# Layers 2 and 3 of a four-layer convolution network: TensorE's products pinned to alternate between pairs of the two layers

## The chip, the cores and the metric

The kernel runs on one core of one Trainium2 chip. The metric is the device time of one execution in microseconds (us). Names of engines: PE is TensorE's matmuls, PEld its weight loads, DVE is VectorE, ACT ScalarE, POOL GpSimd, SP the engine that issues most transfers. L1002 means line 1002 of the kernel.

## The reference

The input x has the shape (4, 8, 512, 512): four time steps t, eight channels, images of 512 x 512. Four layers follow each other, each of the form x + f(gn(x)), where gn normalises each group of two channels of an image to mean 0 and variance 1.

```python
x = x + _L0_conv_ref(_gn(x), ...)             # spiking attention
x = x + _L1_conv_ref(_gn(x), L1_conv_w)       # 13 x 13 depthwise convolution
x = x + _L2_conv_ref(_gn(x), L2_conv_weight, L2_conv_bias)   # quantised 3 x 3
x = x + _L3_conv_ref(_gn(x), L3_conv_weight, L3_conv_bias)   # plain 3 x 3
```

Only layers 2 and 3 matter here. Layer 2 rounds its normalised input to integers between -127 and 127, convolves it with rounded weights and scales the result back:

```python
qx = _quantize(x, sx); qw = _quantize(weight, sw)
out = conv3x3(qx, qw) / (sx * sw) + bias
```

Layer 3 is `conv3x3(gn(x), weight) + bias`. Its normalisation needs the mean and variance over the whole image of layer 2's output at this t, so layer 3 of a t can only begin when layer 2 of that t is done.

## The kernel before

Layers 0 and 1 run first and leave their result in device memory (x2d). The function `layers23` then does layers 2 and 3 together. An image of 512 rows is cut into 85 windows of 8 rows, with 8 channels each: 64 partitions hold one window, 128 hold two. A tile k is up to two windows; a *pair* p is two such tiles, so up to four windows. There are 22 pairs in each t (`N_PAIRS`), 88 in all, and the last pair of a t is smaller.

One loop, over n, goes through all pairs. Iteration n does, in the order of the program:

- `load`: the transfer of pair n+5 into SBUF, on SP's queue;
- `normalise` of pair n+2: POOL copies x into u in another order of columns (L967), ACT normalises it into y (L971);
- `quantise` of pair n+1: DVE rounds y into xq (L982), one of three buffers;
- `layer2` of pair n: for each of the two tiles six products of 64 x 64 by 64 x 512 in bf16 (L1002) into one of three PSUM buffers; then DVE scales them and adds u, writing layer 2's output into the ring x3 (L1009), and either ACT squares it with a running sum (L1015) or DVE takes its statistics (L1020);
- from time to time `halos`: transfers on POOL's queue inside x3, which give each window the border rows of its neighbours (L1154);
- `layer3` of pair n-25 (22 pairs of one t plus `LAG` = 3): POOL fills two edge columns (L1097), PE does 24 products of 64 x 64 by 64 x 512 in f32 (L1104) into two of four PSUM buffers, ACT adds the constant (L1113), and SP stores the output (L1120).

The ring x3 holds 26 pairs (`RING`). Pair n of layer 2 is written where pair n-26 was, so the eviction at L1009 may not start before layer 3 has read pair n-26. That is a dependency that the framework finds by itself.

After the last pair of a t the steps of `norm3` are spread over the next iterations: sums on DVE, two products that add over partitions (L178, in `group_steps`), a power on POOL (L195), the scaled weights of layer 3 (L1073), and a product that gives its constant (L1082).

Each engine works through its own queue in a fixed order. The framework sets that order when the program is built, from the order of the program and an estimate of when each instruction becomes ready, so instructions may stand in another order than they are written in. `tc.issue_after(op)` ties this down: each instruction traced in the block stands behind `op` on the engine of `op`. It adds no semaphore and no wait for another engine. In the kernel before, `normalise` and `quantise` stand behind the last DVE and ACT operations of the layer 2 before (the dictionary `done`), layer 2 stands behind `normalise` and `quantise` on their own engines, and layer 3's products stand behind layer 2's of the same iteration (`did`). Nothing ties layer 2's products of the next iteration to layer 3's of this one.

Of the kernel before, what the change touches and what calls it, by code (L numbers as in the profile page):

```python
# [78 lines left out]
def windows(k):  # L79

    p, j = divmod(k, 2)
    every = [(a, 4 * p + 2 * j + (a ^ j)) for a in range(2)]
    return [(a, q) for a, q in every if q < W_ALL]
# [813 lines left out]
def layers23(  # L897
    s, tc, x2d, out, ident, ind, mask2, avg_same, group_steps, m2, r2, most, w, early, pool
):
    nc = tc.nc  # L900
# [36 lines left out]
    def tiles(p):  # L937
        return [k for k in (2 * p, 2 * p + 1) if k < W2_N]

    def slot(t, p):  # L940
        return 2 * ((t * N_PAIRS + p) % RING)
# [3 lines left out]
    def load(t, p):  # L945
        ahead[t, p] = xt = early["x"].tile([P, 2, D], F32, tag="x", name=f"x2_{t}_{p}")
        src = x2d[t]
        first, second = (dict(windows(k)) for k in (2 * p, 2 * p + 1))
        for a, q in first.items():

            n = 2 if a in second else 1
            step = second[a] - q if n == 2 else 1
            nc.sync.dma_start(
                xt[a * HALF : (a + 1) * HALF, :n, :],
                bass.AP(
                    src.tensor, src.offset + q * W_STEP * B * D,
                    [[D, HALF], [step * W_STEP * B * D, n], [1, D]],
                ),
            )

    def normalise(t, p):
        n, n_p = len(tiles(p)), HALF * len(windows(tiles(p)[-1]))
        x = ahead.pop((t, p))[:n_p, :n, :]
        u = early["u"].tile([P, 2, D], F32, tag="u", name="u2")
        y = early["y"].tile([P, 2, D], F32, tag="y", name="y2")
        for j in range(n):
            nc.gpsimd.tensor_copy(  # L967
                u[:n_p, j, :].rearrange("p (v g) -> p v g", g=PH),
                x[:, j, :].rearrange("p (g v) -> p v g", g=PH),
            )  # L970
        op = nc.scalar.activation(  # L971
            y[:n_p, :n, :], u[:n_p, :n, :], AF.Identity, bias=w["mr"][:n_p, t : t + 1],
            scale=w["r"][:n_p, t : t + 1],
        )
        ready[t, p] = u, y[:n_p, :n, :]
        return op.ins

    def quantise(t, p):
        u, y = ready[t, p]
        n_p, n, _ = y.shape  # L980
        xq = w["xq"][(t * N_PAIRS + p) % 3]
        op = nc.vector.tensor_scalar(  # L982
            xq[:n_p, :n, 2 : D + 2], y, ROUND, ROUND, op0=ALU.add, op1=ALU.subtract
        )
        ready[t, p] = u, xq
        return op.ins
# [4 lines left out]
    def layer2(t, p):  # L991
        ks = tiles(p)
        n_p = HALF * len(windows(ks[-1]))
        u, xq = ready.pop((t, p))
        s0 = slot(t, p)
        st3 = w["st3"][t % 2]
        for j, k in enumerate(ks):
            ps = ps_2.tile([P, D], F32, tag="conv2", name="ps_conv2")
            for dx in range(3):
                for a, _ in windows(k):  # L1000
                    half = slice(a * HALF, (a + 1) * HALF)
                    mm = nc.tensor.matmul(  # L1002
                        ps[half, :], lhsT=w["band2"][half, 0, dx, :], rhs=xq[half, j, dx + 1 : dx + 1 + D],
                        start=dx == 0, stop=dx == 2,
                    )
            own = x3[:n_p, s0 + j, 1 : D + 1]
            sums = w["sums"][t % 2][:, :, k : k + 1]
            summed = k in by_sums(t)
            done["DVE"] = nc.vector.scalar_tensor_tensor(  # L1009
                own, ps[:n_p, :], w["inv"][:n_p], u[:n_p, j, :], op0=ALU.mult, op1=ALU.add,  # L1010
                accum_out=sums[:, 0, :] if summed else None,
            ).ins
            if summed:
                square = wpool.tile([P, D], BF16, tag="square", name="square")
                done["ACT"] = nc.scalar.activation(  # L1015
                    square, own, AF.Square, bias=w["m"][:, t : t + 1], scale=-1.0,
                    accum_out=sums[:, 1, :],
                ).ins
            else:
                done["DVE"] = nc.vector.bn_stats(st3[:n_p, k, :], own).ins  # L1020
        return mm.ins
# [3 lines left out]
    def halos(t, p0, p1):  # L1025


        for c in range(4):
            first = max(p0, 1) if c == 0 else p0
            n = min(p1, (W_ALL - c + 3) // 4) - first  # L1030
            _, j, a = place(c)
            before, j_b, a_b = place(c + 3)
            for q0, q1, n_q in split(t, first, n, before - 1):
                here = pairs[a * HALF : (a + 1) * HALF, q0 : q0 + n_q, j, :]
                there = pairs[a_b * HALF : (a_b + 1) * HALF, q1 : q1 + n_q, j_b, :]
                end = (W_IN - 1) * B
                yield here[:B], there[W_STEP * B : (W_STEP + 1) * B]
                yield there[end : end + B], here[B : 2 * B]
# [51 lines left out]
    def layer3(t, p, zero, band, const):  # L1090


        ks = tiles(p)
        s0 = slot(t, p)
        n_p = HALF * len(windows(ks[-1]))
        edge = x3[:n_p, s0 : s0 + len(ks), 0 : D + 2 : D + 1]
        nc.gpsimd.tensor_copy(edge, zero[:n_p].unsqueeze(2).to_broadcast([n_p, len(ks), 2]))  # L1097
        ps = [ps_3.tile([P, D], F32, tag="conv3", name="ps_conv3") for _ in ks]
        for dx in range(3):
            for j, k in enumerate(ks):  # L1100
                for a, q in windows(k):
                    half = slice(a * HALF, (a + 1) * HALF)
                    b = 1 if q == W_ALL - 1 else a ^ j
                    nc.tensor.matmul(  # L1104
                        ps[j][b * HALF : (b + 1) * HALF, :], lhsT=band[half, b, dx, :],
                        rhs=x3[half, s0 + j, dx : dx + D],
                        start=dx == 0, stop=dx == 2,
                    )
        for j, k in enumerate(ks):
            q = 4 * p + 2 * j  # L1110
            used = slice(HALF if q == W_ALL - 1 else 0, P)
            o = early["o"].tile([P, D], F32, tag="o", name="o3")
            nc.scalar.activation(o[used], ps[j][used], AF.Identity, bias=const[used])  # L1113
            row, n = q * W_STEP + 1, 2 * W_STEP
            at = 2 * B
            if q == 0:
                row, n, at = row - 1, n + 1, at - B
            if q == W_ALL - 1:
                n, at = W_STEP + 1, HALF
            nc.sync.dma_start(  # L1120
                out[t, :, row : row + n, :].rearrange("c r w -> r c w"), o[at : at + n * B, :]
            )

    n_chunk = N_PAIRS // 2
    copies, at_once = [], 0
    n_all = T * N_PAIRS
    norms, norm, done = {}, iter(()), {}
    for n in range(n_all + N_PAIRS + LAG):  # L1130
        if n < n_all:
            for m in range(6) if n == 0 else [n + 5]:
                if m < n_all:
                    load(*divmod(m, N_PAIRS))


            with ExitStack() as order:
                for op in done.values():
                    order.enter_context(tc.issue_after(op))
                for m in range(3) if n == 0 else [n + 2]:  # L1140
                    if m < n_all:
                        first = normalise(*divmod(m, N_PAIRS))
                for m in range(2) if n == 0 else [n + 1]:
                    if m < n_all:
                        then = quantise(*divmod(m, N_PAIRS))
            with tc.issue_after(first), tc.issue_after(then):
                did = layer2(*divmod(n, N_PAIRS))
        next(norm, None)
        if n_chunk < n <= n_all + 3 and n % n_chunk == 3:
            t, p = divmod(n - 3 - n_chunk, N_PAIRS)  # L1150
            copies = list(halos(t, p, p + n_chunk))
            at_once = -(-len(copies) // (n_chunk - 2))
        for _ in range(min(at_once, len(copies))):
            nc.gpsimd.dma_start(*copies.pop(0))  # L1154
        if n >= N_PAIRS + LAG:
            t, p = divmod(n - N_PAIRS - LAG, N_PAIRS)
            with tc.issue_after(did):
                layer3(t, p, *norms[t])
        if n < n_all and n % N_PAIRS == N_PAIRS - 1:
            norm = norm3(n // N_PAIRS)  # L1160
        next(norm, None)
# [36 lines left out]
```

## Time and profile before

| | |
|---|---|
| time, median of 3 | 3056.27 us (3052.8 to 3060.18) |
| profiled span | 3049.7 us |
| layer 0 | 0 to about 2116 us |
| layer 1 | 2116 to about 2595 us |
| layer 2 alone (25 pairs) | 2595 to 2678 us |
| layers 2 and 3 together | 2678 to 2970 us |
| layer 3 alone (25 pairs) | 2970 to 3049.7 us |
| PE busy over the span | 2917.8 us, 96% |
| DVE, ACT, POOL busy | 73%, 18%, 34% |

The page cuts the span into 40 equal slices of about 76 us; each digit is the busy share of a slice in tenths. Shares over the whole span hide the stage in question, since layer 0 alone takes two thirds of it; the views that count are those by stretches of time. The DMA share is the mean busy share of the core's 16 DMA engines. A wait is written as "engine, what waited, <- what released it: total us, times, longest us".

### The profile page before, as it was taken

To read this page: it belongs to the slowest core of one execution; us is meant where nothing else is said; L and a number is where in the kernel's file an instruction comes from. 1 tells how busy PE (TensorE), PEld (TensorE's weight loads), DVE (VectorE), ACT (ScalarE), POOL (GpSimd) and SP (SyncE) were. 2 spreads that over 40 slices of the span, in tenths; PEclk is the share of its full clock that TensorE was granted. 3 is DMA by queue.
4 is the path that set the end of the run, shared out by engine and by line. 5 is a ranking of instruction groups with operands and counts; after the bars stand their busy time and mean duration, and the time that the engine had idled before them with its cause. 6 is when DMAs were issued, how large, how long until landed. Compare 5 with 4: busy or idle time off the path is not lost. (4 is left out here: it accounts for less than half of the span.)

```text
span 3049.7 us, 38814 instructions
## 1 busy us (share of the span) xinstructions
PE 2917.8 (96%) x13993; PEld 1459.2 (48%) x13993; DVE 2223.0 (73%) x3793; ACT 554.2 (18%) x867; POOL 1042.9 (34%) x1963
## 2 busy tenths in 40 slices
PE   8999999999999999999999999998999999678989
PEld 6555555555555555555555555554433333234434
DVE  5997688688779868868876876886455556967860
ACT  1400010010000001000001000100111111756664
POOL 1242233333234323323322432333111112766751
PEclk9999999999999999999999999998999999799999
DMA  5222222222222222122221111112877878888986
GB/s 181 80 81 64 77 63 64 70 63 70 70 63 63 71 65 76 60 67 63 63 70 43 57 50 50 57 36 73 212 215 204 217 202 226 147 181 203 229 189 160
DMA packets 275702, 327.37 MB, mean 107 GB/s; under 512 B 23600, under 2 KB 171192, under 8 KB 275285
## 3 DMA queue, kind: packets, MB, share of 16 engines
q1 hardware_dynamic: 211930, 235.77, 29.0%
q0 software_dynamic: 23776, 62.35, 7.5%
q10 hardware_dynamic: 39803, 26.77, 3.0%
q8 instruction: 110, 1.80, 0.3%
q14 instruction: 83, 0.68, 0.1%
HBM read 210.60 MB, written 103.17 MB: 103 GB/s over the span
## 5 line engine op out<-in xcount | busy, mean ns | idle before, releaser
L464 PE MATMUL ps_in<-w_v,xn 128*128 128x512 f32 x1024 | 461.4, 599 | 2.4 <-issue 2.1
L464 PE MATMUL ps_in<-w_k,xn 128*128 128x512 f32 x1024 | 450.2, 593 | 1.1 <-DVE v_k L429 0.8
L464 PE MATMUL ps_in<-xn,w_q 128*128 128x512 f32 x1024 | 449.6, 592 | 0.1
L750 PE MATMUL ps_conv<-x,bt 112*64 112x512 f32 x2048 | 444.5, 593 | 0.0
L500 PE MATMUL ps_b<-toep,vtok 128*64 128x512 bf16 x3072 | 369.8, 381 | 0.0
L412 ACT ACTIVATE h_q<-v_q,c_half 128x512 f32<-128x512 f32 x96 | 69.3, 722 | 1543.6 <-DVE v_q L408 1184.1
L549 POOL COPY x1s<-x1s 128x2 f32<-128x2 f32 (+1 forms) x1024 | 226.7, 275 | 296.0 <-DVE x1s L538 296.0
L437 POOL TENSOR_TENSOR h_v<-h_v,c_v 128x512 f32<-128x512 f32 x96 | 123.1, 1282 | 575.3 <-DVE h_v L436 540.7
L527 PE MATMUL ps_out<-wp,so 128*128 128x512 f32 x1024 | 308.9, 444 | 0.0
L464 PEld LDWEIGHTS ps_in<-w_k,xn 128*128 128x128 f32 x1024 | 194.1, 190 | 222.5 <-issue 205.0
L464 PEld LDWEIGHTS ps_in<-xn,w_q 128*128 128x128 f32 x1024 | 191.8, 190 | 220.0 <-issue 213.1
L464 PEld LDWEIGHTS ps_in<-w_v,xn 128*128 128x128 f32 x1024 | 190.0, 190 | 216.4 <-issue 210.9
L750 PEld LDWEIGHTS ps_conv<-x,bt 112*64 112x64 f32 x2048 | 149.9, 135 | 286.0 <-issue 285.5
L500 PEld LDWEIGHTS <-vtok 128*64 128x64 bf16 x3072 | 208.6, 110 | 123.1 <-issue 1.6
L1104 PE MATMUL ps_conv<-x,band_t 64*64 64x512 f32 x2040 | 265.9, 609 | 0.0
L967 POOL COPY u<-x 128x512 f32<-128x512 f32 (+1 forms) x172 | 203.9, 1219 | 109.3 <-issue 66.2
L527 PEld LDWEIGHTS ps_out<-wp,so 128*128 128x128 f32 x1024 | 192.6, 188 | 94.1 <-issue 58.3
L1002 PE MATMUL ps_conv<-xq,band 64*64 64x512 bf16 x1020 | 144.9, 409 | 65.6 <-DVE xq L982 53.6
L538 DVE SCALAR_TENSOR_TENSOR x1s<-v_p,xr 128x256 f32<-128x256 f32 x256 | 186.6, 769 | 14.9 <-DMA x<-x1s 3.6
L766 POOL DMA_DIRECT2D x<-xo x128 | 71.4, 564 | 339.9 <-ACT xo L757 325.4
L1009 DVE SCALAR_TENSOR_TENSOR x<-ps_conv,inv,u 128x512 f32<-128x512 f32 (+1 forms) x172 | 123.1, 743 | 84.6 <-PE ps_conv L1104 64.4
L195 POOL TENSOR_TENSOR grstd_x<-grstd_x,neg_half 128x1 f32<-128x1 f32 (+1 forms) x28 | 22.3, 796 | 462.2 <-DVE grstd_x L194 462.2
(182 smaller groups left out, 3609.4 us busy)
## 6 DMA issues: line engine op xcount, KB each, us to landing
x<-x SPq DMA_DIRECT2D x64, 917.0 KB
x<-x SPq DMA_DIRECT2D x168, 256.0 KB
x<-x1s POOLq DMA_DIRECT2D x128, 262.0 KB, 2.6
x<-in_x SPq DMA_DIRECT2D x128, 256.0 KB
xr<-in_x SPq DMA_DIRECT2D x128, 256.0 KB
out<-o SPq DMA_DIRECT2D x164, 192.0 KB
xs<-in_x SPq DMA_DIRECT2D x112, 256.0 KB
x<-xo ACTq DMA_DIRECT2D x128, 128.0 KB
```

The lines of the kernel that those rows point to most:

```text
L437: nc.gpsimd.tensor_add(h, h, c_twice[n])
L464: mm = nc.tensor.matmul(ps, lhsT=lhsT, rhs=rhs, start=k == 0, stop=k == NC - 1)
L500: nc.tensor.matmul(pb[two * DH : (two + 1) * DH, :], lhsT=v[:, c, h * DH : (h + 1) * DH], rhs=toep[z][:, h, u : u + N], start=c == 0 and z ...
L527: nc.tensor.matmul(ps, lhsT=so[:, k, c * P : (c + 1) * P], rhs=wpT[z][:, k, :], start=k == 0 and z == 0, stop=k == NC - 1 and z == 1,)
L538: nc.vector.scalar_tensor_tensor(own, v.rearrange("p (g v) -> p g v", g=PH)[:, two, :], 1.0, by_phase[:, two, :], op0=ALU.is_ge, op1=ALU.add,)
L549: nc.gpsimd.tensor_copy(x1[:, f, u : u + n], x1[:, fm, um - n + 1 : um + 1][:, ::-1])
L750: nc.tensor.matmul(ps[q * M1 : (q + 1) * M1, :], lhsT=bt[:, z, :], rhs=xt[:, w0 : w0 + N_PS1, z : z + NV], start=z == 0, stop=z == SHIFTS - 1,
L766: engine.dma_start(bass.AP(dst.tensor, dst.offset + (q * n_half * W1_OUT * B + b) * D + f * NV, [[B * D, W1_OUT], [W1_OUT * B * D, n_half] ...
L967: nc.gpsimd.tensor_copy(u[:n_p, j, :].rearrange("p (v g) -> p v g", g=PH), x[:, j, :].rearrange("p (g v) -> p v g", g=PH),)
L1002: mm = nc.tensor.matmul(ps[half, :], lhsT=w["band2"][half, 0, dx, :], rhs=xq[half, j, dx + 1 : dx + 1 + D], start=dx == 0, stop=dx == 2,)
L1009: done["DVE"] = nc.vector.scalar_tensor_tensor(own, ps[:n_p, :], w["inv"][:n_p], u[:n_p, j, :], op0=ALU.mult, op1=ALU.add, accum_out=sums[ ...
L1104: nc.tensor.matmul(ps[j][b * HALF : (b + 1) * HALF, :], lhsT=band[half, b, dx, :], rhs=x3[half, s0 + j, dx : dx + D], start=dx == 0, stop= ...
```

## The change

Layer 3 now returns its last product, and layer 2's instructions of the next iteration are traced behind it, in addition to `normalise` and `quantise`. Since layer 3 was already tied behind layer 2 of its own iteration, PE's products of this stage are now in one fixed order: the pair of layer 2 of iteration n, the pair of layer 3 of iteration n, the pair of layer 2 of iteration n+1, and so on. Only PE's queue is bound by it. In the first 25 iterations there is no layer 3 yet and `behind` is empty. The purpose is to keep PE from running layer 2 ahead of layer 3.

```diff
@@ layer3
-                    nc.tensor.matmul(
+                    mm = nc.tensor.matmul(
                         ps[j][b * HALF : (b + 1) * HALF, :], lhsT=band[half, b, dx, :],
...
                 out[t, :, row : row + n, :].rearrange("c r w -> r c w"), o[at : at + n * B, :]
             )
+        return mm.ins
@@ the loop over n
-    norms, norm, done = {}, iter(()), {}
+    norms, norm, done, behind = {}, iter(()), {}, ()
...
-            with tc.issue_after(first), tc.issue_after(then):
+            with ExitStack() as order:
+                for op in (first, then, *behind):
+                    order.enter_context(tc.issue_after(op))
                 did = layer2(*divmod(n, N_PAIRS))
...
             with tc.issue_after(did):
-                layer3(t, p, *norms[t])
+                behind = (layer3(t, p, *norms[t]),)
```

## The prediction

> **What bounds the kernel now.** I read the page first: its 40 slices show PE at 9 nearly everywhere, except in the last part of the span.
>
> ```profile
> PE   8999999999999999999999999998999999678989
> DMA  5222222222222222122221111112877878888986
> ```
>
> The dip is the stage that the change touches. Layer 2 starts at 2595 us; its first 25 pairs run alone. From 2678 to 2970 us pairs of layer 2 and of layer 3 share PE, and the last 25 pairs of layer 3 run alone to 3049.7. Nothing before 2678 is touched, and the tail is one product after another on PE (70.5 us busy of 79.7), so the change can only move the 292 us between. The second view is the busy time by stretch: us, then PE, PEld, DVE, ACT, POOL busy, the granted clock, the DMA share and GB/s.
>
> ```profile
> 2687.00:2725.00 38.00, 25.49 (x188) 10.37 (x189) 16.27 (x30) 18.05 (x30) 15.94 (x20) 0.91 0.79 174
> 2725.00:2768.00 43.00, 43.00 (x401) 20.53 (x399) 36.00 (x59) 34.00 (x55) 36.96 (x50) 1.00 0.86 200
> ...
> 2903.00:2930.00 27.00, 18.75 (x156) 8.43 (x160) 11.24 (x21) 13.55 (x21) 13.15 (x16) 0.97 0.91 208
> 2930.00:2970.00 40.00, 40.00 (x366) 18.36 (x359) 29.07 (x54) 28.37 (x48) 22.68 (x34) 0.98 0.80 169
> ...
> 2678.00:2970.00 292.00, 251.36 (x2174) 118.81 (x2166) 206.22 (x351) 186.94 (x300) 188.43 (x247) 0.97 0.88 200
> ```
>
> The reader is to see two regimes. In the first and third line PE is busy two thirds of the time while DVE, ACT and POOL are busy less than half: nobody is full, so a chain of waits sets the pace. In the second and fourth PE is full. Over all 292 us PE is idle for 40.6. The third view, PE's waits in this stretch, says on what:
>
> ```profile
> PE ps_conv L1002 <- DVE xq L982: 22.3, 22, 1.6
> PE ps_conv L1002 <- DVE x L1009: 12.0, 14, 1.0
> PE gps_x L178 <- DVE gsum_x L175: 5.0, 2, 2.6
> ```
>
> So 34.3 us stand before products of layer 2, and about 6 us (with 1.3 of a smaller group) before those of the statistics. The fourth view, the chain that ended last in order of time, shows one turn of the slow regime:
>
> ```profile
> 2820.33 0.62 PE ps_conv L1002 x4
> 2820.95 0.21 PE ps_conv L1104
> 2821.17 2.69 PE ps_conv L1104 x22
> 2823.86 0.03 issue
> 2823.89 0.77 DVE x L1009
> 2824.66 0.02 issue
> 2824.68 0.69 DVE st L1020
> 2825.37 0.66 DVE x L1009 x2
> 2826.03 0.62 DVE xq L982
> 2826.65 0.04 issue
> 2826.69 0.62 PE ps_conv L1002 x4
> ```
>
> From 2820.33 to 2826.69 is 6.36 us for one pair of each layer, in strict series: layer 3, then DVE's eviction of layer 2 (L1009), its statistics, the second eviction, the next quantisation (L982), then PE again. The eviction waits for layer 3 because it writes into x3, a ring of 26 slots: pair n of layer 2 takes the slot of pair n-26, which layer 3 must have read. PE has run layer 2 two pairs ahead: at 2683.56 it begins pair 28 of layer 2 (counting the products from 2595) when pair 1 of layer 3 is still to come, and the eviction of pair 27, which needs the slot of pair 1, waits for it. The quantisation of pair 29 is queued behind that eviction. After one iteration in which two pairs of layer 3 run together (46 products at 2725.51) the lead is gone and the timeline repeats every 3.875 us without a gap: 12 products of layer 2 and 24 of layer 3.
>
> **What the skill says.** "TensorE: Matmul & The Clock Gate", section "Step-by-step: what each phase is for", says that matmuls stay in program order and only weight loads are pulled ahead. The trace agrees: the 0.93 us wait of layer 2's second tile at 2818.34 is followed by nothing else on PE, though layer 3 had work. So PE's order is worth something. "SBUF — State Buffer", section "Who interferes with whom", says that a two-port VectorE operation and GpSimd take a shared port pair in turns. The trace agrees: L982 takes 0.69 us beside an idle POOL and 1.2 us and more beside POOL's copies (median 1.08, maximum 3.35). "DMA: Bandwidth & Descriptors", section "Issuing engines are not separate DMA queues", says that all queues run on the same 16 engines; here loads and stores on SP's queue and the halos on POOL's share a mean of 0.88. "Perfetto Trace Analysis", section "Identifying the Most-Contended Engine", warns that DMA occupancy misleads; the trace agrees, with a share of 1.03 at only 164 GB/s from 2630 to 2677. So I use the share as a soft limit.
>
> **The change part by part.**
> 1. Returning layer 3's last matmul and holding it in `behind`: no instruction and no semaphore. Cost nothing, as it is a bound on the order of one engine's own queue.
> 2. Layer 2's products of pair n+1 stand behind layer 3's of iteration n. Then PE runs 12 and 24 in turn, and the eviction of pair n finds pair n-26 already read, since that came before pair n's own products. The ring's wait (64.0 us of DVE in this stretch) goes, and with it the 34.3 us of PE. I count all of it as removed from PE's path. Nor do the other buffers take its place: PSUM of layer 2 has three buffers, so the second tile of pair n+1 needs only the first eviction of pair n, which has the 2.6 us of layer 3 to finish its 0.74; xq has three too.
> 3. What is queued behind the new place: if pair n's xq is late, layer 3 of iteration n and all after it wait. Per pair DVE needs 2 x 0.743 + 0.69 + 0.08 + 1.20 = 3.46 us, ACT 1.21 + 2 x 0.68 + 0.72 + 0.19 = 3.48, POOL 2 x 1.225 + 0.22 + 0.61 = 3.28: all under 3.875, and the 43 us stretches with PE full show that they fit.
> 4. At the two ends of a t in this stretch layer 3 of the next t waits for its statistics. In before, 3 pairs of each layer covered that chain (2767.73 to 2781.67) and PE lost 3.3 us. Four iterations, 15.5 us, now lie between; I keep 8 us for the two ends together, at 0 to 16.
> 5. The granted clock was 0.97 here, and 0.91 in the slow regime; without gaps I give back 0.02 x 251 = 5 us, at 0 to 7.
>
> PE alone would thus gain 40.6 - 8 + 5 = 38 us. But the transfers then have to fit into less time. A share of 0.88 over 292 us is 257 us of all 16 engines. In the last 27 us (2943 to 2970) the loads are over and PE was full, so nothing is won there. In the 265 us before, the share was 0.89, or 236 us of work, which depends on the data and not on the order. The fullest long stretch was 2827 to 2903: 0.94 and 225 GB/s over 76 us; the densest short one was 1.03. If it can hold 0.94, 236/0.94 = 251 us, a gain of 14; at 1.00 a gain of 29; at 1.03, 36. I take 0.97, midway between 0.94 and 1.00: 236/0.97 = 243, a gain of 22 us. That is less than the 38 of PE, so the transfers end last: 3056 - 22 = 3034 us.
>
> **The rivals.**
> - PE stays the bound: 3056 - 38 = 3018 us. For it: PE was full for 43, 43 and 40 us at shares of only 0.80 to 0.93, and SP's queue waited for data 113 of 292 us. Against it: in the first two of these stretches some 17 loads were issued where 22 were used up, so they lived on loads made ahead.
> - The transfers already set the pace: in the slow stretch 2903 to 2930 the share is 0.91 and SP waits for others only 1.7 us of 27. At 0.90 the 236 us need 262, a gain of 3; with a part of it lost elsewhere I set 3051 us. Against it: from 2687 to 2725 the share was 0.79, with room.
> - Slower: the rigid order lets a late xq or a late norm hold both layers. With 12 us more at each of the two ends and the transfers at 0.90, 3056 - 3 + 24 = 3077 us. For it: POOL already stands 7.5 us before a power (L195) at one end, and its copies feed xq. Against it: the longer cover of point 4.
>
> **How the numbers follow.** Forecast (3026 to 3043) 0.42; PE the bound 0.25; pace of the transfers 0.21, half of it still over 6 us faster; slower 0.12. Faster by over 0.2% (below 3050.2): 0.42 + 0.25 + 0.10 = 0.77; within: 0.11; slower: 0.12. The range runs from 3012, PE with smaller losses at the ends than I kept, to 3056, which leaves out most of the last case.
>
> **What would show it.** Right: PE's timeline in the stage shows 12 and 24 in turn; the wait of L1009 on L1104 falls from 64 us to a few; PE's two waits of layer 2 fall from 34.3 to 10 or 15, now on a quantisation that itself waits for loads; the stretch of both layers takes about 270 us at a share near 0.95. Wrong in size: a stretch of about 254 us (PE the bound) or 285 and more with POOL waiting long for loads. Wrong altogether: L1009 still waits for L1104, or the gaps at the ends of a t grow beyond 8 us each.

## The result and the profile after

The changed kernel takes 3031.15 us (3029.82 to 3032.56, 4 runs) against 3055.07 us of the kernel before in the same comparison. The ratio is 0.9919 with a 95% interval of 0.9902 to 0.9937, so it is faster by 0.6 to 1.0%, about 24 us. The forecast was 3034 us. The profiles show one execution of each kernel, and these two lie closer together than the medians: 3051.45 and 3032.56 us.

The page's slices of the changed kernel, PE and the DMA share:

```profile
PE   8999999999999999999999999999899999688989
DMA  5222222221212222222221111111877878698986
```

The dip in the last part is shallower by little. The busy time by stretch tells more. The stretch of both layers is measured here from the first product of layer 3 to the last of layer 2, and the tail from there to 5 us before the end of the span, where the last products end. Of the kernel before (us, then PE, PEld, DVE, ACT, POOL busy, granted clock, DMA share, GB/s):

```profile
2677.60:2968.15 290.55, 249.91 (x2157) 118.28 (x2156) 204.88 (x346) 186.22 (x298) 188.82 (x248) 0.97 0.88 200
2968.15:3044.70 76.55, 72.33 (x621) 34.12 (x613) 6.91 (x27) 35.30 (x53) 13.91 (x42) 0.98 0.64 169
```

Of the changed kernel, with the first part of the stretch on its own ahead:

```profile
2675.66:2747.00 71.34, 71.34 (x660) 34.90 (x660) 59.23 (x102) 55.49 (x91) 57.59 (x77) 0.99 1.02 211
...
2675.66:2956.76 281.10, 250.26 (x2193) 118.14 (x2193) 200.12 (x357) 188.29 (x304) 190.72 (x255) 0.97 0.92 210
2956.76:3025.80 69.04, 68.76 (x599) 26.24 (x591) 5.10 (x19) 34.56 (x52) 11.72 (x37) 1.00 0.66 179
```

The two profiled spans differ by 18.9 us (3049.7 and 3030.8): layer 3 starts 1.9 us earlier, the stretch is 9.4 us shorter, and the tail 7.5. For the first 71 us of the stretch PE now runs without a gap, where it had gone through turns of 6.3 us until 2725. After that it waits again, 30.8 us in all, but elsewhere. PE's waits in the stretch after the change:

```profile
PE ps_conv L1104 <- POOL x L1097: 14.3, 6, 6.5
PE ps_conv L1104 <- ACT o L1113: 13.4, 13, 2.2
PE ps_conv L1104 <- issue: 1.9, 1, 1.9
PE gps_x L178 <- DVE gsum_x L175: 0.9, 2, 0.6
```

The 34.3 us ahead of layer 2's products are gone, and so is the wait for the ring. In their place layer 3 waits for its edge columns (L1097) and for its PSUM to be emptied (L1113). The waits of the other engines say why. DVE's wait for the ring in the kernel before:

```profile
DVE x L1009 <- PE ps_conv L1104: 64.0, 18, 5.3
```

In the changed kernel:

```profile
POOL u L967 <- DMA x<-x: 60.9, 22, 7.8
ACT o L1113 <- DMA out<-o: 59.9, 35, 4.2
...
DVE x L1009 <- PE ps_conv L1104: 1.4, 2, 0.9
```

The wait of L1009 on L1104 has fallen from 64.0 to 1.4 us. POOL waits 60.9 us for loads to land, and ACT 59.9 us for stores to give back output tiles. The kernel before has neither of these two waits in its stretch. POOL stood still before the same copies there too, 57.5 us, but the profile shows nothing that it waited for. How such a wait reaches PE is seen in the timeline of the changed kernel (start, us, engine, line):

```profile
2893.40 1.47 PE L1002 MATMUL ps_conv<-xq,band 64*64 64x512 bf16 x12
...
2898.55 2.04 POOL L967 COPY u<-x 128x512 f32<-128x512 f32 x2 [7.82 <-DMA x<-x]
...
2900.53 0.57 POOL L1158 DMA_DIRECT2D x<-x  x1
...
2901.09 0.20 POOL L1097 COPY x<-zero 128x4 f32<-128x4 f32 x1
...
2901.35 4.84 PE L1104 MATMUL ps_conv<-x,band_t 64*64 64x512 f32 x24 [6.48 <-POOL x L1097]
```

POOL sits 7.82 us before a copy whose load is late. Behind it in POOL's queue stand a halo and the 0.20 us of the edge columns, so layer 3 waits 6.48 us for them. In PE's records after this gap 24 products take 4.84 us rather than 2.8. From 2886.74 us on SP's queue is 8.06 us in issuing four loads, where the median of one load in the stretch is 0.63 us, and over 2886 to 2890 the DMA share is only 0.64. Late issue, and not full engines, may thus be behind this wait.

### The profile page after: what moved, and what is told of

The parts are those of the page before. It is cut to its first block, busy times and chain, and to the rows that moved or that the text cites. A ratio compares the mean times of both kernels' runs of the same rounds, so it can differ in the third digit from the quotient of the medians.

```text
span 3030.8 us, 38824 instructions
## 1 busy us (share of the span) xinstructions
PE 2915.8 (96%) x13993; PEld 1450.6 (48%) x13993; DVE 2212.7 (73%) x3793; ACT 553.9 (18%) x867; POOL 1039.8 (34%) x1963
## 5 line engine op out<-in xcount | busy, mean ns | idle before, releaser
L1104 PE MATMUL ps_conv<-x,band_t 64*64 64x512 f32 x2040 | 271.7, 609 | 30.2 <-POOL x L1097 14.3
L1104 PEld LDWEIGHTS ps_conv<-x,band_t 64*64 64x64 f32 x2040 | 105.1, 135 | 145.5 <-issue 93.7
L757 ACT ACTIVATE xo<-ps_conv,off 128x512 f32<-128x512 f32 x128 | 88.0, 688 | 445.8 <-PE ps_conv L750 387.0
```

The source lines that it names most:

```text
L757: nc.scalar.activation(xo[:, a, :], ps, AF.Identity, bias=off[:, t : t + 1])
L1104: mm = nc.tensor.matmul(ps[j][b * HALF : (b + 1) * HALF, :], lhsT=band[half, b, dx, :], rhs=x3[half, s0 + j, dx : dx + D], start=dx == 0, ...
```

## The experiments

Theory: before the change PE ran layer 2 two pairs ahead, so the eviction into the ring waited for layer 3; the pin takes that wait away, and then the transfers end last. The rivals: the fixed order helps for a reason of its own; or what is left is set by POOL, DVE, ACT or the ends of a t. All ratios are to the kernel before, run in the same comparison.

**A ring one slot longer, PE's order left free.**

```diff
-RING = 23 + LAG
+RING = 24 + LAG
-        "o": ctx.enter_context(pool("o3", 10, side="right")),
+        "o": ctx.enter_context(pool("o3", 8, side="right")),
```

> The kernel before, with PE's order left free; the ring x3 has 27 slots in place of 26, and the output tiles 8 buffers in place of 10 to make room. Theory (the eviction waits for its slot in the ring because PE is two pairs ahead): with one slot more the eviction of pair n needs layer 3 of pair n-27, which PE has already done, so the wait of L1009 on L1104 falls from 64 us to under 10 and the time comes to 3028 to 3038 us, as with the pin. Rival (what helps is the fixed order itself, the ring is incidental): no gain, 3050 to 3058 us.

Measured: 3031.13 us, ratio 0.9927 (0.9911 to 0.9944). One slot more does what the pin does, without touching PE's order by hand. The wait in question, in this kernel's stretch:

```profile
DVE x L1009 <- PE ps_conv L1104: 10.0, 13, 3.3
```

It is 10.0 us, at the edge of what was expected, in place of 64.0. PE begins the stretch two pairs ahead as in the kernel before, but a turn now takes 4.33 us (2692.11 to 2696.44) in place of 6.3. The ring was the cause, and the order alone is not what helps. This run also has two output buffers fewer, which make the room for the slot.

**The pin loosened by one iteration.**

```diff
-                behind = (layer3(t, p, *norms[t]),)
+                recent.append(layer3(t, p, *norms[t]))
+                behind = tuple(recent[-2:-1])
```

> The changed kernel with the pin loosened by one iteration: layer 2 of iteration n+1 stands behind layer 3 of iteration n-1, so PE may be one pair ahead, but not two. Theory (only a lead of two pairs meets the ring): no wait of L1009 on L1104 in the slow series, 3027 to 3037 us. Rival (strict alternation is needed): the slow turns of 6.3 us come back, 3045 to 3056 us.

Measured: 3030.21 us, ratio 0.9918 (0.9903 to 0.9933). Strict alternation isn't needed; a lead of one pair is harmless. The expectation of no wait at all was too strong, as the lines of this kernel show:

```profile
DVE x L1009 <- PE ps_conv L1104: 24.8, 16, 1.9
...
PE ps_conv L1002 <- DVE x L1009: 3.5, 13, 0.3
PE ps_conv L1104 <- POOL x L1097: 3.0, 3, 2.0
PE ps_conv L1002 <- DVE xq L982: 1.3, 3, 0.8
```

DVE does wait for the ring, 24.8 us, but only 3.5 and 1.3 us of waits ahead of layer 2 reach PE. A wait counts by what it holds up. The waits for transfers say the same: with the longer ring POOL waits 8.3 us for loads and ACT 19.1 for stores, with the loosened pin 24.0 and 32.3, against 60.9 and 59.9 with the pin, and the three times are alike. Whether the transfers hold these two kernels as well was not tested.

**Half of the stores left out, before and after the change.** The second tile of each pair is computed and not stored.

```diff
+            if j == 1:
+                continue
             nc.sync.dma_start(
                 out[t, :, row : row + n, :].rearrange("c r w -> r c w"), o[at : at + n * B, :]
```

In the kernel before:

> The kernel before, with the stores of each pair's second tile left out (half of the output is not written), so about a third of the stage's bytes on SP's queue. Theory (the slow turns hang on the ring, not on transfers): the turns of 6.3 us stay, the wait of L1009 on L1104 stays at 55 to 70 us, 3045 to 3056 us. Rival (transfers already set the pace before the change): 3030 us or less.

Measured: 3053.98 us, ratio 0.9997 (0.9989 to 1.0006). Half of the stores gone, and no time gained. The ring's wait of this kernel is where it was:

```profile
DVE x L1009 <- PE ps_conv L1104: 65.8, 18, 5.3
```

So the transfers did not set the pace before the change. In the changed kernel:

> The changed kernel with the same half of the stores left out. Theory (after the change the transfers end last; PE alone would give 38 us): POOL's wait for loads falls from 61 us to under 20, PE's idle time in the stretch of both layers from 29 us to about 10, 3010 to 3022 us. Rival (what is left is set by POOL, DVE and ACT, or by the ends of a t): 3027 to 3033 us, unchanged.

Measured: 3003.31 us, ratio 0.9829 (0.9814 to 0.9844), 7 us below the range that was expected. The same stores left out, worth nothing before, are worth 28 us now. Its stretch, and all of PE's waits in it:

```profile
2675.70:2928.70 253.00, 243.35 (x2194) 126.09 (x2194) 217.64 (x360) 188.77 (x304) 199.45 (x255) 0.97 0.90 192
```

```profile
PE gps_x L178 <- DVE gsum_x L175: 5.1, 2, 2.6
PE ps_conv L1104 <- ACT square L1015: 4.6, 2, 2.3
```

PE waits 9.7 us, all of it at the two ends of a t. No wait for a load or a store is left among the waits of this stretch. The rival that POOL, DVE and ACT set the rest falls: they do the same work here, and PE is held only at the ends. The DMA share is 0.90 here, where no transfer holds PE, and 0.92 in the changed kernel: the share alone does not tell the two apart.

**The halos left out,** another kind of transfer.

```diff
-            nc.gpsimd.dma_start(*copies.pop(0))
+            copies.pop(0)
```

> The changed kernel with the halos left out (the border rows of the windows stay as they are, so layer 3 is wrong there). It takes away 23.4% of 276 us = 65 us of all 16 engines, another kind of transfer than the stores that were left out before, and 0.61 us of POOL for each. Theory (throughput): with 254 - 65 = 189 us of transfers PE ends last, the stretch of both layers takes 248 to 258 us, 3003 to 3015 us. Rival (stores and output tiles alone hold the loads back): 3022 to 3031 us.

Measured: 2995.55 us, ratio 0.981 (0.9795 to 0.9825). The stretch of this kernel:

```profile
2671.27:2920.78 249.51, 240.50 (x2192) 120.19 (x2196) 211.93 (x361) 185.74 (x301) 154.50 (x161) 0.99 0.73 209
```

It is 249.5 us, inside the 248 to 258; the total lies 7 us below the range, in part because layer 3 also starts 4.4 us earlier. Leaving out two different kinds of transfer brings the stretch to 250 to 253 us, the length that PE alone was reckoned to need. The stores free SP's queue and output tiles, the halos free 36 us of POOL (154.50 in place of 190.72); what the two have in common is fewer bytes for the DMA engines. The rival that stores and output tiles alone hold the loads back falls, since the halos touch neither. That a part of this second gain comes from POOL's freed time was not tested.

**Where the transfers' wait shows up.** Two kernels give it room in one place. The edge columns filled by DVE:

```diff
-        nc.gpsimd.tensor_copy(edge, zero[:n_p].unsqueeze(2).to_broadcast([n_p, len(ks), 2]))
+        nc.vector.tensor_copy(edge, zero[:n_p].unsqueeze(2).to_broadcast([n_p, len(ks), 2]))
```

> The changed kernel with the two edge columns of layer 3 filled by DVE in place of POOL, so that they no longer stand in POOL's queue behind copies that wait for loads. Theory (the throughput of the transfers ends last; the place of the edges only decides where PE waits): PE's wait of L1104 on the edges (14.3 us) goes and a wait for xq or for the output tiles takes its place, 3025 to 3033 us. Rival (the edges' place in the queue costs PE those 14 us): 3013 to 3021 us.

Measured: 3034.32 us, ratio 0.9929 (0.9912 to 0.9945). PE's wait on the edges is one piece of 5.2 us, and this has come instead:

```profile
PE ps_conv L1002 <- DVE xq L982: 22.4, 8, 4.5
```

No gain from it; the time lies 1 us above the range of the theory. But POOL's wait for loads is only 10.7 us and ACT's for stores 10.4 here, and the DMA share 0.88, so this run speaks against the rival (the place of the edges costs 14 us) without speaking for the transfers. More than the place of the edges changed, too: that piece of 5.2 us stands ahead of layer 3's first product, which comes 4.7 us later than in the changed kernel (2680.37). The loads one pair further ahead:

```diff
-            for m in range(6) if n == 0 else [n + 5]:
+            for m in range(7) if n == 0 else [n + 6]:
-        "x": ctx.enter_context(pool("x2", 6, side="right")),
+        "x": ctx.enter_context(pool("x2", 7, side="right")),
-        "o": ctx.enter_context(pool("o3", 10, side="right")),
+        "o": ctx.enter_context(pool("o3", 8, side="right")),
```

> The changed kernel with the loads one pair further ahead (7 buffers of x, load of pair n+6) and, to make room, 8 buffers of output tiles in place of 10. Theory (throughput): the loads come no faster, 3027 to 3036 us, slightly worse where the stores have less room. Rival (the loads are issued too late, latency): POOL's wait for loads falls by half, 3012 to 3022 us.

Measured: 3028.45 us, ratio 0.9914 (0.9899 to 0.9929), not to be told from the changed kernel. In its stretch POOL has no wait for loads any more, and PE waits for the other side of the same engines:

```profile
ACT o L1113 <- DMA out<-o: 58.2, 37, 5.5
...
PE ps_conv L1104 <- ACT o L1113: 19.0, 15, 3.9
```

The rival got its sign, the wait for loads gone, but not its time. This run has two output buffers fewer as well. ACT's wait for stores was 59.9 us with all ten, so it did not grow, but PE's wait on ACT did, from 13.4 to 19.0. With this and the loosened pin together:

> Both looser forms together: PE may be one pair ahead (as in the run with slack 1), loads one pair further ahead, 8 buffers of output tiles. Theory (the transfers' throughput ends last, so more room on either side buys only what is lost at the ends of a t): 3024 to 3031 us. Rival (the two kinds of room add up): 3015 to 3022 us.

Measured: 3032.84 us, ratio 0.9926 (0.9914 to 0.9939), 2 us above what was expected and no better than either alone. The two kinds of room do not add up.

**Transfers issued from other queues.** The stores from ACT's queue, `nc.scalar.dma_start` in place of `nc.sync.dma_start` at the store of layer 3:

> The changed kernel with the stores issued from ACT's queue in place of SP's, so that loads no longer wait behind a store whose tile isn't ready. Theory (the 16 engines are shared, so the throughput stays, and ACT, at 3.5 us of 3.9 a pair, pays for the issues): 3030 to 3050 us. Rival (SP's queue, not the engines, holds the loads back): 3010 to 3022 us.

Measured: 3084.99 us, ratio 1.0096 (1.0081 to 1.0111). The halos from SP's queue, `nc.sync.dma_start` in place of `nc.gpsimd.dma_start`:

> The changed kernel with the halos issued from SP's queue in place of POOL's software queue. POOL is freed of 0.61 us each, and the halos' packets go through the hardware queue. Theory (throughput of the engines ends last, and the halos' packets took 65 of the stage's 254 us of all engines in the kernel before): if their packets get cheaper the time falls to 3010 to 3024 us, if not 3028 to 3045 us, since SP then waits for evictions ahead of its loads. Rival (POOL's own time ends last): under 3022 us with the halos' share unchanged.

Measured: 3111.48 us, ratio 1.0185 (1.0164 to 1.0207). Both are far worse than either theory said. With the stores on ACT, DVE's wait for y (L971, on ACT) in the stretch rises from 30.9 to 115.3 us: the 119 issues stand between ACT's operations, and at their median of 0.78 us they come to 93 us, which with ACT's 191.9 us of work is 285 of the 313.7 us of the stretch (an estimate from these figures). With the halos on SP the DMA share falls to 0.71 over a stretch of 338 us, which is 240 us of all engines where the changed kernel has 0.92 of 281, or 259. So the transfers took less of the engines, and the time was lost all the same: POOL's wait for loads is 103.1 us. In SP's one queue the loads now stand behind 65 halo issues at a median of 0.75 us, about 49 us, and behind stores that wait 106 us for ACT's output tiles, where they wait 71 in the changed kernel. The halos themselves wait only 6 us there. Which of these makes the loads late was not tested.

## Why the prediction was right, and where its sizes were off

- *The ring is the cause of the slow turns.* Shown: the wait of L1009 on L1104 goes from 64.0 to 1.4 us with the pin and to 10.0 with one slot more.
- *PE alone would gain 38 us, a stretch of about 254.* Shown for the stretch by the two kernels with fewer transfers, 253 and 249.5 us. Their totals, 3003 and 2996 us, lie below the 3018 reckoned for this case, since the start and the tail gained as well.
- *The transfers end last.* Shown in that leaving transfers out is what helps: half of the stores are worth 1 us before, within the interval, and 28 us after. Not shown is that the 16 engines were full, as the sum by shares supposed. From 2747 to 2934 us, where most of PE's waits are, the share was 0.89, as much as in the kernel before while its loads ran. Whether loads come late because the engines are taken or because SP's queue issues them late, as at 2886.74, stays open: the runs that moved transfers to other queues lost time on the way.
- *The stretch's gain of 22 us.* Too large: 9.4 us in the profiles, or about 13 for the same work, since the stretch now holds one more pair of each layer (2193 of PE's records in place of 2157, 3.9 us at the full pace). Ahead of layer 3's first product stand 26 pairs of layer 2 in place of 27 (not 25, as the table above has it), and 587 products of layer 3 in place of 609 are left for the tail. The mis-sized term is the share that the 16 engines hold, put at 0.97 over the part with loads; it came to 0.93 there (2675.66 to 2934). PE was full for the first 71 us at a share of 1.02, which the loads made ahead probably allowed; afterwards waits for loads and stores came one after another. And the last part, after the loads, was reckoned as full on PE; it lost 4.6 of 23.2 us to waits for ACT to empty PSUM (L1113).
- *The tail and the start, put at nothing.* "The change can only move the 292 us between" was wrong. The tail is 7.5 us shorter. PE's idle time in it falls by 3.9 (4.2 before, all at the last end of a t; 0.3 after), and 22 products fewer are about 2.5; the rest goes with a mean clock of 1.00 in place of 0.98. The start gives 1.9 us, with the pair of layer 2 that now stands behind layer 3's first. Taken over both layers, from 2595 us to the last product, PE has 3092 records in either kernel; its idle time falls from 77.6 to 60.8 us and its busy time by 2.1, together the 18.9 us.
- *The total.* That 3031 us came out for 3034 forecast is in part luck: a stretch that gained too little and a tail and a start that gained something nearly cancel. The 281 us of the stretch, with POOL waiting 60.9 us for loads, are closer to the forecast's own sign of being wrong in size (285 and more) than to its 270.
- *Ends of a t at 8 us.* In the changed kernel's timeline the gaps there are 3.6 and 4.6 us, together 8.2. Only 0.9 of it stands before the products of the statistics and 5.4 before ACT has emptied PSUM, so the sum is right and its parts are not those meant.
- *The clock, 5 us given back.* Not in the stretch, where the mean clock is 0.97 before and after: gaps remained, and over 2865 to 2906, around the gap shown above, it was 0.92. With fewer transfers PE's busy time in the stretch was 243 and 240.5 us in place of 250.
- *Where PE would wait.* Wrong in place: not ahead of layer 2 on a late quantisation, where nothing is left, but ahead of layer 3, on edge columns queued behind POOL's wait for loads and on output tiles not yet stored.
- *L982 "beside an idle POOL".* The reading is too simple. In the slow turns POOL's copy begins 0.2 us after L982, and L982 still takes 0.69 us (as at 2689.14). Only where a copy was already running did it mostly take 1.2 us and more.

## What to carry to other kernels

An engine that runs ahead of its partner in a ring can be the one that stalls the ring: the cure is a bound on the lead, or one slot more, and either gave about 24 us here. Before counting a removed wait as a gain, add up the transfers of the stretch and ask what share they would need in the shorter time, but take that share as a rough sign only. Then test it with a pair of runs: the same transfers left out of the kernel before and of the one after show which of the two they hold.

## What the runs showed of the hardware

The mean busy share of the 16 DMA engines is no limit at 1, and no measure of whether transfers hold PE: it stood at 1.02 over 71 us with PE full, at 0.90 in the stretch where none of PE's waits was for a transfer (half of the stores left out), and at 0.92 in the changed kernel. Nor does it follow the bytes: without halos the stretch moved 209 GB/s at a share of 0.73, with them 210 GB/s at 0.92.

Issuing the same transfers from another engine's queue cost 29 us (stores on ACT) and 55 us (halos on SP) against the kernel before, more than the 24 us that the pin won, though the halos' run took less time of the DMA engines.
